# Computing an expert router's gates for three tiles at a time instead of tile by tile

## The chip, the cores and the metric

The kernel runs on one core of a Trainium2 chip. All arithmetic is in float32. The metric is the time of one execution on the device in microseconds (us), the median of several runs. The engines are called as in the profile: PE (TensorE, matrix products), DVE (VectorE), ACT (ScalarE), POOL (GpSimd) and SP (SyncE, which here only issues transfers).

## The reference, cut to what matters

Two layers run on 1024 tokens of 1024 channels each (4 images of 16 by 16). Layer 0 is a convolution-like attention with relative positions. Layer 1 is a causal attention followed by a mixture of eight experts. Only the mixture matters here:

```python
gate_logits = softmax(x @ gate_w + gate_b)            # x: 1024 normalised tokens, 8 experts
selected = gate_logits >= 0.1
weights = gate_logits * selected
weights = weights / where(sum(weights) == 0, 1, sum(weights))
out = sum over e of weights[:, e] * (x @ expert_w[e] + expert_b[e])
```

The kernel does not run every token through every expert. It makes, for each expert, a list of the tokens that chose it, with their weights, gathers those tokens' rows, multiplies them with the expert's matrix and adds the weighted result to the output rows.

## The kernel before, in words

The 1024 tokens are 8 tiles of 128 (`NT = 8`, `P = 128`). The part that matters is the end of the attention and the beginning of the experts, where three things are interleaved on the engines by hand (`tc.manual_schedule()`: each engine executes in the order in which the code issues).

**The output projection as a clock.** `project_out(t, j)` (L894) computes half `j` of tile `t` as 8 products of 128x128 by 128x512 (L898), then DVE adds the result to the residual row `xb` (L900). After each product `one_more()` (L1325) raises the counter `chunks`; I call the products chunks and number them as the code does. Chunk 8 is the last product of tile 3's first half, chunks 9 to 16 are tile 3's second half, 17 to 24 and 25 to 32 tile 4, 33 to 48 tile 5, 49 to 64 tile 6, 65 to 80 tile 7. At a given chunk the table `after` (L1301) starts stages of the gating of earlier tiles:

- stage 0, `normalise` (L1117): layer norm of the tile's rows on DVE and ACT (a square root, L134), and for tiles 0 to 5 a way through memory and back on SP's queue that puts the row into the order that a DVE transpose needs. Tiles 6 and 7 are transposed on PE instead.
- stage 1, `turn_rows` (L1140): the transpose (L179 on DVE, or L1149 on PE with copies L1150 on ACT).
- stage 2, `gate_sums` (L1159): 8 small products into `parts` (L1163), and a DVE copy `sums` (L1165).
- stage 3, `gate` (L1168): one product `pg` (L1171) that adds the four partial sums, then DVE adds the bias and takes the maximum, and ACT makes the exponentials (L1180).
- stage 4, `thresholds` (L1183): ten small DVE instructions, among them the choice `g_keep` (L1188).
- stage 5, `place` (L1197): two products `pp` (L1201, L1202) count, for each token and expert, how many tokens were kept before it (`kept` is the running count over tiles, L1203); DVE turns the count into a list position (L1207 to L1213) and into two 0/1 tables `one` (L1216). Products of one table with token and weight, `entry` (L1224), are made by POOL, for tiles 6 and 7 by DVE.
- stage 6, `enter` (L1233): 8 small products add the tile's entries to `lists` in PSUM (L1235).

**Around tile 7 and the start of the experts.** After chunk 80 the list of expert 0, which doesn't need tile 7, is copied (L1246), spread (L1255) and taken as gather indices (`take_lists`, L1274 to L1277). POOL then issues the gathers of expert 0's rows, four per 128 slots (`fetch`, L1010). Meanwhile `weighted` (L1018) runs tile 7 through expert 0's matrix as it stands: 16 products `dense_pe` (L1025), with tile 7's own stages 2 to 5 at places named in a dictionary (L1528 to L1535). DVE makes the sums that the expert's products need: `T` from the weights (L1384, L1387, L1394), `A`, the transposed gathered rows (L179), and `S` from A (L152 to L155). Each pair of 128 slots is computed with seven half-size products instead of eight (`products`, L1427; L1441). Tile 7's `enter` stands between product 2 and product 3 of expert 0's first pair (L1557), and after product 4 the other seven lists are spread and taken (`last_lists`, L1354).

Tiles in PSUM named by `tr` and `mm` rotate over three banks each, so a product may also wait until the third tile before it has been read.

Of the kernel before, what the change touches and what calls it, by code (L numbers as in the profile page):

```python
# [32 lines left out]
F32 = mybir.dt.float32  # L33
# [6 lines left out]
P = 128  # L40
C = 1024
# [28 lines left out]
def kernel(  # L70
# [57 lines left out]
    def tr(name):  # L128
        return ps.tile([P, HALF], F32, tag="tr", name=name)
# [937 lines left out]
    with ExitStack() as gating:  # L1067
# [38 lines left out]
        nc.vector.memset(ones, 1.0)  # L1106
        kept = l2.tile([P, E], F32, tag="kept", name="kept")
        nc.vector.memset(kept, 0.0)
        kept_short = l2.tile([P, 2], F32, tag="kept_short", name="kept_short")

# [47 lines left out]

        def gate_sums(t, row_T):  # L1159

            parts = tr(f"parts{t}")[:, :P]
            for c in range(NC):
                nc.tensor.matmul(parts[ts(c % Q, 32), :], gw[:, c, :], row_T[:, c, :], start=(c < Q), stop=(c >= Q))  # L1163
            sums = l2w.tile([P, P], F32, tag="parts", name=f"sums{t}", bufs=1)
            nc.vector.tensor_copy(sums, parts)  # L1165
            return sums

        def gate(t, sums):  # L1168

            pg = tr(f"pg{t}")  # L1170
            nc.tensor.matmul(pg[:, :E], sums, quarters, start=True, stop=True)  # L1171
            listed = small.tile([P, E, 2], F32, tag="listed", name=f"listed{t}")
            nc.vector.tensor_copy(listed[:, :, 0], token[:, t : t + 1].to_broadcast([P, E]))
            weight = listed[:, :, 1]
            top = small.tile([P, 1], F32, tag="g_top", name=f"g_top{t}")
            fix = small.tile([P, 1], F32, tag="g_fix", name=f"g_fix{t}")
            keep = small.tile([P, E], F32, tag="g_keep", name=f"g_keep{t}")
            nc.vector.tensor_add(weight, pg[:, :E], gb)
            nc.vector.tensor_reduce(top, weight, AX.X, ALU.max, negate=True)
            nc.scalar.activation(weight, weight, AF.Exp, bias=top)  # L1180
            return listed, top, fix, keep

        def thresholds(listed, top, fix, keep):  # L1183
            weight = listed[:, :, 1]
            nc.vector.tensor_reduce(top, weight, AX.X, ALU.add)
            nc.vector.reciprocal(top, top)
            nc.vector.tensor_scalar(weight, weight, top, None, ALU.mult)
            nc.vector.tensor_scalar(keep, weight, THRESHOLD, None, ALU.is_ge)  # L1188
            nc.vector.tensor_mul(weight, weight, keep)
            nc.vector.tensor_reduce(top, weight, AX.X, ALU.add)  # L1190
            nc.vector.tensor_scalar(fix, top, 0.0, None, ALU.is_equal)
            nc.vector.tensor_add(top, top, fix)
            nc.vector.reciprocal(top, top)
            nc.vector.tensor_scalar(weight, weight, top, None, ALU.mult)
            return listed, keep

        def place(t, listed, keep):  # L1197


            pp = tr(f"pp{t}")  # L1200
            nc.tensor.matmul(pp[:, :E], before, keep, start=True, stop=False)  # L1201
            nc.tensor.matmul(pp[:, :E], ones, kept, start=False, stop=True)  # L1202
            nc.vector.tensor_add(kept, kept, keep)  # L1203
            if t == NT - 2:
                nc.vector.tensor_copy(kept_short, kept[:, :: E - 1])
            slot = small.tile([P, E], F32, tag="place", name=f"place{t}")
            nc.vector.tensor_scalar(slot, keep, -1.0, 1.0, ALU.mult, ALU.add)  # L1207
            nc.vector.tensor_mul(slot, slot, from_end[:, t, :])
            nc.vector.tensor_add(slot, slot, pp[:, :E])
            at = small.tile([P, 3, E], I32, tag="at", name=f"at{t}")  # L1210
            nc.vector.tensor_copy(at[:, 0, :], slot)
            nc.vector.tensor_scalar(at[:, 1, :], at[:, 0, :], 31, None, ALU.bitwise_and)
            nc.vector.tensor_scalar(at[:, 2, :], at[:, 0, :], 5, None, ALU.logical_shift_right)  # L1213
            row, column = (l2w.tile([P, E, 32], F32, tag=f"one{i}", name=f"one{i}_{t}") for i in range(2))
            for i, one in enumerate((row, column)):
                nc.vector.tensor_tensor(  # L1216
                    one,
                    count32.unsqueeze(1).to_broadcast([P, E, 32]),
                    at[:, 1 + i, :].unsqueeze(2).to_broadcast([P, E, 32]),
                    ALU.is_equal,  # L1220
                )
            entry = l2w.tile([P, E, 2, 32], F32, tag="entry", name=f"entry{t}")
            for i in range(2):
                (nc.vector if t >= NT - 2 else nc.gpsimd).tensor_mul(  # L1224
                    entry[:, :, i, :], column, listed[:, :, i].unsqueeze(2).to_broadcast([P, E, 32])
                )
            return row, entry
# [53 lines left out]

        normal, turned_rows, summed, gated, placed = {}, {}, {}, {}, {}

        def stage(n, t):
            if n == 0:
                normal[t] = normalise(t)
            elif n == 1:
                turned_rows[t] = turn_rows(t, normal[t])
            elif n == 2:
                summed[t] = gate_sums(t, turned_rows[t])  # L1290
            elif n == 3:
                gated[t] = gate(t, summed[t])
            elif n == 4:
                gated[t] = thresholds(*gated[t])
            elif n == 5:
                placed[t] = place(t, *gated[t])
            else:
                enter(t, *placed[t])


        after = {  # L1301
            0: (8, 16, 18, 19, 20, 24, 29),
            1: (8, 23, 26, 27, 28, 32, 37),
            2: (19, 30, 33, 34, 35, 39, 44),
            3: (27, 38, 40, 41, 42, 46, 51),
            4: (34, 47, 50, 51, 52, 56, 61),
            5: (50, 61, 63, 64, 66, 69, 74),
            6: (65, 69, 71, 72, 73, 76, 80),
        }
# [15 lines left out]
        def one_more():  # L1325
            nonlocal chunks
            chunks += 1
            for t in after:
                for n, at in enumerate(after[t]):
                    if at == chunks:  # L1330
                        stage(n, t)
            others.get(chunks, lambda: None)()
# [21 lines left out]
        def last_lists(entries):  # L1354
            take_lists(1, E, spread_lists(1, entries))


            pn = tr("pn")
            nc.tensor.matmul(pn[:, :E], ones, kept, start=True, stop=True)
            need = l2.tile([P, E], F32, tag="need", name="need")  # L1360
            nc.vector.tensor_copy(need, pn[:, :E])
            pn0 = tr("pn0")
            nc.tensor.matmul(pn0[:, :2], ones, kept_short, start=True, stop=True)
            nc.vector.tensor_scalar(need[:, :: E - 1], pn0[:, :2], float(LEFT), None, ALU.add)
            most = l2.tile([P, 1], F32, tag="most", name="most")
            nc.vector.tensor_reduce(most, need, AX.X, ALU.max)
            nc.vector.tensor_copy(most_i, most)
# [25 lines left out]
        def fourth_sum(e):  # L1393
            nc.vector.tensor_sub(T[e][2], half(e, 1, 0), T[e][1])  # L1394
# [120 lines left out]
        with tc.manual_schedule():  # L1515
# [3 lines left out]
            for k in range(3):  # L1519
                get(0, k)  # L1520
            y = weighted(
                lambda: gated[NT - 1][0][:, 0, 1:2],
                turned_rows[NT - 1],
# [4 lines left out]
                {  # L1528
                    (0, 3): lambda: stage(2, NT - 1),
                    (0, 4): lambda: (stage(3, NT - 1), first_sum(0)),  # L1530
                    (0, 5): lambda: stage(4, NT - 1),
                    0: lambda: (stage(5, NT - 1), put(0, 0)),
                    (1, 3): lambda: put(0, 1),
# [11 lines left out]
            for e in range(E):  # L1545
# [10 lines left out]
                if e == 0:  # L1556
                    between[2] = lambda: (stage(6, NT - 1), fourth_sum(0), put(0, 2))  # L1557
                    between[3] = lambda: (entries.append(copy_lists(1)), put(0, 3))
# [27 lines left out]
                else:  # L1586
                    between = {
                        1: lambda: nc.sync.dma_start(last_rows[0], out[ts(NT - 1, P), :]),
                        4: lambda: nc.vector.scalar_tensor_tensor(
                            last_rows[0], bias[e], gated[NT - 1][0][:, e, 1:2], last_rows[0], ALU.mult, ALU.add  # L1590
                        ),
# [4 lines left out]
            for j in range(2):  # L1596
# [5 lines left out]
                y = last_rows[0][:, ts(j, HALF)]  # L1602
                nc.vector.scalar_tensor_tensor(y, pe, gated[NT - 1][0][:, E - 1, 1:2], y, ALU.mult, ALU.add)
                nc.sync.dma_start(out[ts(NT - 1, P), ts(j, HALF)], y)
# [69 lines left out]
```

## Time and profile before

| | us |
|---|---|
| median of 3 runs (lowest, highest) | 1237.75 (1236.86, 1240.2) |
| the profiled execution's own time | 1237.34 |
| its span in the profile | 1235.5 |

| stage (us from the span's start) | length | PE busy | DVE busy | ACT busy | POOL busy |
|---|---|---|---|---|---|
| chunks 8 to 80, 661.47 to 742.42 | 80.95 | 78.59 | 57.23 | 28.29 | 9.66 |
| tile 7 and its 16 products, 742.42 to 764.90 | 22.48 | 19.51 | 14.01 | 5.71 | 14.34 |
| expert 0's first five products and the lists, 764.90 to 785.33 | 20.43 | 19.11 | 17.67 | 1.45 | 7.51 |
| the rest, 785.33 to 1235.50 | 450.17 | 444.59 | 255.78 | 57.42 | 204.30 |

The granted PE clock is 1.00 in all four. A row of the timeline gives the start and the length in us, the engine, the source line, the operation, out<-in and the number of merged instructions; in square brackets stands how long the engine was idle before it, and what ended that. A float32 product appears as two records on PE, so "x2" is one product. The end of a product is modelled, and includes a tail that overlaps the next one.

### The profile page before, as it was taken

To read this page: it belongs to the slowest core of one execution; us is meant where nothing else is said; L and a number is where in the kernel's file an instruction comes from. 1 tells how busy PE (TensorE), PEld (TensorE's weight loads), DVE (VectorE), ACT (ScalarE), POOL (GpSimd) and SP (SyncE) were. 2 spreads that over 40 slices of the span, in tenths; PEclk is the share of its full clock that TensorE was granted. 3 is DMA by queue.
4 is the path that set the end of the run, shared out by engine and by line. 5 is a ranking of instruction groups with operands and counts; after the bars stand their busy time and mean duration, and the time that the engine had idled before them with its cause. 6 is when DMAs were issued, how large, how long until landed. Compare 5 with 4: busy or idle time off the path is not lost.

```text
span 1235.5 us, 13332 instructions
## 1 busy us (share of the span) xinstructions
PE 1219.3 (99%) x4796; PEld 631.7 (51%) x4796; DVE 740.5 (60%) x1333; ACT 219.8 (18%) x514; POOL 409.6 (33%) x470
## 2 busy tenths in 40 slices
PE   9999999999999999999999999999999999999998
PEld 5445884788874444444444444444344434434443
DVE  5796636757323666657554867666656556565642
ACT  3310111130001222222222332101201111111110
POOL 0041341354000222223240106436452645363521
PEclk9999999999999999999999999999999999999999
DMA  9002024771220635253483547373855576556442
GB/s 350 23 1 80 7 48 140 254 260 50 68 68 5 180 100 172 91 170 116 134 267 133 205 171 255 89 218 89 239 147 156 111 230 163 152 137 182 100 83 54
DMA packets 94121, 169.77 MB, mean 137 GB/s; under 512 B 11968, under 2 KB 48848, under 8 KB 94048
## 3 DMA queue, kind: packets, MB, share of 16 engines
q1 hardware_dynamic: 75680, 112.68, 28.0%
q0 software_dynamic: 16144, 51.45, 17.4%
q10 hardware_dynamic: 2224, 4.72, 1.1%
q8 instruction: 40, 0.66, 0.2%
q14 instruction: 33, 0.27, 0.1%
HBM read 116.12 MB, written 48.50 MB: 133 GB/s over the span
## 4 chain that ended last, share of the span: by engine, by line
PE 70%; issue 13%; POOL 5%; DMA 4%; DVE 4%; SPq 2%; ACT 1%; POOLq 0%; DVEq 0%; ACTq 0%
PE p L1441 31%; PE pv L657 7%; PE po L898 6%; POOL s_q L855 5%; PE pq_pair L392 4%; PE left L1483 3%; PE pq L311 3%; PE pqk L657 3%; PE pk L423 2%; DMA ln_rows<-ln_rows 2%; PE rest L1497 2%; PE pv L530 2%; PE pT L502 2%; SPq L479 2%; DMA s<-two_T 1%
## 5 line engine op out<-in xcount | busy, mean ns | idle before, releaser
L1010 POOL DMA_INDIRECT w_e_xg<-rows,gather x146 | 156.6, 1073 | 57.3 <-issue 42.0
L1441 PE MATMUL p<-w_e,A 128*128 128x512 f32 x368 | 163.2, 593 | 1.3 <-DVE slot L1276 1.3
L855 POOL TENSOR_TENSOR s_q<-s_q,total 128x128 f32<-128x128 f32 (+1 forms) x128 | 66.0, 546 | 276.8 <-DVE total L852 276.8
L898 PE MATMUL po<-w_p,y_T 128*128 128x512 f32 x256 | 118.5, 605 | 0.0
L1033 POOL DMA_INDIRECT out_dram<-y,add x32 | 57.3, 1792 | 177.6 <-ACT y L1447 113.0
L1441 PEld LDWEIGHTS p<-w_e,A 128*128 128x128 f32 x368 | 69.6, 190 | 89.9 <-issue 89.7
L1441 PE MATMUL p<-T,S 128*128 128x512 f32 x256 | 112.7, 593 | 0.0
L1447 ACT ACTIVATE y<-y,slot 128x512 f32<-128x512 f32 x64 | 46.1, 722 | 330.8 <-DVE y L1455 176.2
L841 ACT ACTIVATE s_q<-s,top 128x256 f32<-128x256 f32 (+1 forms) x128 | 56.6, 443 | 186.3 <-issue 146.9
L657 PE MATMUL pqk<-ln,w_qk 128*128 128x512 f32 x192 | 85.6, 595 | 0.0
L1441 PEld LDWEIGHTS p<-T,S 128*128 128x128 f32 x256 | 48.6, 190 | 60.8 <-issue 60.5
L898 PEld LDWEIGHTS po<-w_p,y_T 128*128 128x128 f32 x256 | 45.9, 190 | 47.9 <-issue 46.9
L179 DVE STREAM_TRANSPOSE A<-w_e_xg 128x1024 f32<-128x1024 f32 x32 | 39.6, 1238 | 48.3 <-DMA w_e_xg<-rows,gather 48.3
L657 PE MATMUL pqk<-T,S_qk 128*128 128x512 f32 x128 | 58.5, 599 | 0.0
L657 PEld LDWEIGHTS pqk<-ln,w_qk 128*128 128x128 f32 x192 | 36.0, 190 | 43.3 <-issue 42.3
L1441 PE MATMUL p<-w_e,S 128*128 128x512 f32 x128 | 57.5, 592 | 0.0
L1441 PE MATMUL p<-T,A 128*128 128x512 f32 x128 | 57.5, 592 | 0.0
L311 PE MATMUL pq<-w_q,xn 128*128 128x512 f32 x96 | 44.5, 599 | 0.3 <-ACT xn L291 0.3
L657 PE MATMUL pv<-w_v,ln 128*128 128x256 f32 x192 | 43.5, 380 | 1.1 <-ACT ln L215 1.1
L1483 PE MATMUL left<-w_e,one 128*32 128x512 f32 x312 | 41.8, 593 | 0.0
L1441 PEld LDWEIGHTS p<-w_e,S 128*128 128x128 f32 x128 | 24.3, 190 | 30.6 <-issue 30.4
L1441 PEld LDWEIGHTS p<-T,A 128*128 128x128 f32 x128 | 24.3, 190 | 30.6 <-issue 30.4
(327 smaller groups left out, 1893.3 us busy)
## 6 DMA issues: line engine op xcount, KB each, us to landing
w_e<-in_expert_w_dram SPq DMA_DIRECT2D x14, 2048.0 KB, 14.6
s_rows<-s_q SPq DMA_DIRECT2D x32, 384.0 KB, 2.4
s_rows<-s_rows SPq DMA_DIRECT2D x128, 96.0 KB, 2.4
w_qk<-in_W_attnT_dram SPq DMA_DIRECT2D x8, 1024.0 KB, 5.8
xn<-in_xT_dram SPq DMA_DIRECT2D x8, 512.0 KB, 5.5
w_q<-in_Wq_dram SPq DMA_DIRECT2D x16, 256.0 KB, 7.6
x_at<-in_x_dram POOLq DMA_DIRECT2D x8, 512.0 KB
w_v<-in_W_attnT_dram SPq DMA_DIRECT2D x2, 2048.0 KB, 11.2
```

The lines of the kernel that those rows point to most:

```text
L179: nc.vector.transpose(row_T[:, :, :slots].rearrange("p c (g j) -> p g c j", j=32), row[:, : slots // 32, :].rearrange("p g (c i) -> p g c ...
L311: nc.tensor.matmul(pq, xn[:, c, ts(t, P)], w_q[kc][:, c, :], start=(c == 0), stop=(c == NC - 1))
L392: nc.tensor.matmul(bank, a[:, c, :], b[:, c, :], start=(c == 0), stop=(c == NC // 2 - 1))
L657: nc.tensor.matmul(bank, stationary(c), moving(c), start=(c == 0), stop=(c == NC // 2 - 1))
L841: nc.scalar.activation(blocks(h, qt), s[:, h, cols].rearrange("p (b f i) -> p b f i", f=Q, i=32), AF.Exp, bias=top[:, qt, h : h + 1], accu ...
L855: nc.gpsimd.tensor_mul(blocks(h, qt), blocks(h, qt), total[:, qt, h : h + 1].unsqueeze(2).unsqueeze(3).to_broadcast([P, 1 + qt, Q, 32]),)
L898: nc.tensor.matmul(po, y_T[:, c, ts(t, P)], w_p[j][:, c, :], start=(c == 0), stop=(c == NC - 1))
L1010: nc.gpsimd.indirect_dma_start(out=row[:, g, :], out_offset=None, in_=table[: (TOK - P) * Q, :] if e in SHORT else table, in_offset=bass.I ...
L1033: nc.gpsimd.indirect_dma_start(out=out[: TOK - P, :] if e in SHORT else out, out_offset=bass.IndirectOffsetOnAxis(ap=add[:slots, e, k : k ...
L1441: nc.tensor.matmul(bank, a[:, c, :], b[:, c, :], start=(c == 0), stop=(c == NC // 2 - 1))
L1447: nc.scalar.mul(y[i][:, ts(j, HALF)], y[i][:, ts(j, HALF)], slot[:, e, 1, 2 * pair + i : 2 * pair + i + 1])
L1483: nc.tensor.matmul(bank[ts(i, 32), :], stationary, w[of][j][:, c, :], start=(c == 0), stop=(c == NC - 1))
```

## The change

Stages 2 to 5 are computed once for the tiles 0 to 2, once for 3 to 5, and for 6 and 7 alone. The partial sums of three tiles lie side by side in one PSUM bank and are copied at once; `pg` still is one product per tile, into one tile; the DVE instructions work on 24 columns instead of 8; the maximum is subtracted by a DVE instruction, and one exponential serves the three tiles. `kept` becomes a table with a row for each tile (each row is the one before it plus that tile's choice), so that one pair of `pp` products serves the group; these additions now stand ahead of the products. The `one` and `entry` tables become a stage of their own, `entries_of` (stage 6), still tile by tile, and `enter` is stage 7. The table of times is written anew, as `at_chunk`: for a chunk, the pairs (stage, tile) that start after it; it is shown with its lines joined.

```diff
-        def gate_sums(t, row_T):
-            parts = tr(f"parts{t}")[:, :P]
-            for c in range(NC):
-                nc.tensor.matmul(parts[ts(c % Q, 32), :], gw[:, c, :], row_T[:, c, :], start=(c < Q), stop=(c >= Q))
-            sums = l2w.tile([P, P], F32, tag="parts", name=f"sums{t}", bufs=1)
+        def gate_sums(tiles):
+            n = len(tiles)
+            parts = tr(f"parts{tiles[0]}")[:, : n * P]
+            for i, t in enumerate(tiles):
+                for c in range(NC):
+                    nc.tensor.matmul(
+                        parts[ts(c % Q, 32), ts(i, P)], gw[:, c, :], turned_rows[t][:, c, :], start=(c < Q), stop=(c >= Q)
+                    )
+            sums = l2w.tile([P, n * P], F32, tag="ye", name=f"sums{tiles[0]}", bufs=3, padded_shape=[P, C])
             nc.vector.tensor_copy(sums, parts)
...
-        def gate(t, sums):
+        def gate(tiles, sums):
...
             nc.vector.tensor_reduce(top, weight, AX.X, ALU.max, negate=True)
-            nc.scalar.activation(weight, weight, AF.Exp, bias=top)
+            if n == 1:
+                nc.scalar.activation(weight, weight, AF.Exp, bias=top)
+            else:
+                nc.vector.tensor_add(weight, weight, top.unsqueeze(2).to_broadcast([P, n, E]))
+                nc.scalar.activation(weight, weight, AF.Exp)
...
-        def place(t, listed, keep):
-            pp = tr(f"pp{t}")
-            nc.tensor.matmul(pp[:, :E], before, keep, start=True, stop=False)
-            nc.tensor.matmul(pp[:, :E], ones, kept, start=False, stop=True)
-            nc.vector.tensor_add(kept, kept, keep)
+        def place(tiles, listed, keep):
+            n, t0 = len(tiles), tiles[0]
+            for i, t in enumerate(tiles):
+                nc.vector.tensor_add(kept[:, t + 1, :], kept[:, t, :], keep[:, i, :])
+            pp = tr(f"pp{t0}")[:, : n * E]
+            nc.tensor.matmul(pp, before, keep.rearrange("p n e -> p (n e)"), start=True, stop=False)
+            nc.tensor.matmul(pp, ones, kept[:, t0 : t0 + n, :].rearrange("p n e -> p (n e)"), start=False, stop=True)
...
-        after = {
-            0: (8, 16, 18, 19, 20, 24, 29),
-            1: (8, 23, 26, 27, 28, 32, 37),
-            2: (19, 30, 33, 34, 35, 39, 44),
-            3: (27, 38, 40, 41, 42, 46, 51),
-            4: (34, 47, 50, 51, 52, 56, 61),
-            5: (50, 61, 63, 64, 66, 69, 74),
-            6: (65, 69, 71, 72, 73, 76, 80),
-        }
+        at_chunk = {
+            8: ((0, 0), (0, 1)), 16: ((1, 0),), 19: ((0, 2),), 23: ((1, 1),), 27: ((0, 3),), 30: ((1, 2),),
+            33: ((2, 0),), 34: ((0, 4),), 36: ((3, 0),), 38: ((1, 3), (4, 0)), 42: ((5, 0), (6, 0)), 44: ((6, 1),),
+            46: ((7, 0), (6, 2)), 47: ((1, 4),), 48: ((7, 1),), 50: ((0, 5),), 52: ((7, 2),), 61: ((1, 5),),
+            63: ((2, 3),), 65: ((0, 6),), 66: ((3, 3),), 68: ((4, 3),), 69: ((1, 6),), 71: ((2, 6), (5, 3), (6, 3)),
+            73: ((3, 6), (6, 4)), 75: ((7, 3), (4, 6), (6, 5)), 76: ((7, 4),), 77: ((5, 6), (6, 6)), 78: ((7, 5),),
+            80: ((7, 6),),
+        }
...
             y = weighted(
...
-                    (0, 3): lambda: stage(2, NT - 1),
+                    (0, 2): lambda: stage(2, NT - 1),
                     (0, 4): lambda: (stage(3, NT - 1), first_sum(0)),
-                    (0, 5): lambda: stage(4, NT - 1),
-                    0: lambda: (stage(5, NT - 1), put(0, 0)),
+                    (0, 6): lambda: stage(4, NT - 1),
+                    0: lambda: put(0, 0),
+                    (1, 2): lambda: stage(5, NT - 1),
                     (1, 3): lambda: put(0, 1),
...
                 if e == 0:
-                    between[2] = lambda: (stage(6, NT - 1), fourth_sum(0), put(0, 2))
+                    between[2] = lambda: (stage(6, NT - 1), stage(7, NT - 1), fourth_sum(0), put(0, 2))
```

In the last dictionaries the key `(j, c)` means after product `c` of half `j` of tile 7's dense product, a lone key after that half, or after that product of expert 0.

## The prediction

> **What bounds the kernel now.** I read the busy times first, then the chain that ended last, then the timelines of PE, DVE and POOL between 661 and 786 us, where all the edits lie.
>
> ```profile
> PE 1219.3 (99%) x4796; PEld 631.7 (51%) x4796; DVE 740.5 (60%) x1333; ACT 219.8 (18%) x514; POOL 409.6 (33%) x470
> ```
> ```profile
> 885.42 96.33 PE p L1441 x224
> ```
>
> PE is never short of work: time can be won only by taking instructions, or idle time, from PE. In the second line, from the chain, 224 records are 112 products of 512 columns in 96.33 us, 0.86 us each: PE's pace undisturbed. From 785.33 us to the end the chain is PE alone, so whatever is won or lost before that moment is carried unchanged to the end. This is PE before it:
>
> ```profile
> 671.63 0.65 PE L1163 MATMUL parts<-row_T,gw 128*32 128x128 f32 x16 [0.46 <-issue]
> 672.21 1.12 PE L898 MATMUL po<-w_p,y_T 128*128 128x512 f32 x2
> 673.17 0.28 PE L1171 MATMUL pg<-quarters,sums 128*128 128x8 f32 x2
> 673.31 4.54 PE L898 MATMUL po<-w_p,y_T 128*128 128x512 f32 x10
> 677.68 0.28 PE L1201 MATMUL pp<-g_keep,before 128*128 128x8 f32 x2
> 677.82 0.37 PE L1202 MATMUL pp<-kept,ones 128*128 128x8 f32 x2
> 678.04 1.96 PE L898 MATMUL po<-w_p,y_T 128*128 128x512 f32 x4
> ...
> 681.94 0.39 PE L1171 MATMUL pg<-quarters,sums 128*128 128x8 f32 x2 [0.30 <-DVE sums L1165]
> ...
> 690.75 0.39 PE L1171 MATMUL pg<-quarters,sums 128*128 128x8 f32 x2 [0.54 <-DVE sums L1165]
> ...
> 715.59 0.39 PE L1201 MATMUL pp<-g_keep,before 128*128 128x8 f32 x2 [0.34 <-DVE g_keep L1188]
> ...
> 729.51 0.39 PE L1201 MATMUL pp<-g_keep,before 128*128 128x8 f32 x2 [0.50 <-DVE g_keep L1188]
> ...
> 752.92 0.39 PE L1171 MATMUL pg<-quarters,sums 128*128 128x8 f32 x2 [0.75 <-issue]
> ...
> 757.51 0.36 PE L1201 MATMUL pp<-g_keep,before 128*128 128x8 f32 x2 [1.52 <-DVE g_keep L1188]
> ...
> 775.29 0.42 PE L1235 MATMUL lists<-entry,one 128*32 128x64 f32 x12
> ```
>
> The brackets hold the waits at the gates: 2.14 us in the projection's chunks (the first five), 2.27 us beside tile 7 (the last two). The last row has none: tile 7's list entries were ready in time. The distance from one start to the next is what a group costs PE: 0.57 us for the eight `parts`, 0.14 for `pg`, 0.36 for a pair of `pp`.
>
> DVE and POOL beside tile 7 and expert 0's first products:
>
> ```profile
> 754.26 2.28 DVE L1384 TENSOR_TENSOR T<-w_e,w_e 128x2048 f32<-128x2048 f32 x1
> ...
> 759.60 0.81 DVE L1216 TENSOR_TENSOR one<-count,at 128x256 f32<-128x256 int32 x2
> 760.44 0.76 DVE L1224 TENSOR_TENSOR entry<-one,listed 128x256 f32<-128x256 f32 x2
> ...
> 763.61 1.25 DVE L179 STREAM_TRANSPOSE A<-w_e_xg 128x1024 f32<-128x1024 f32 x1 [0.69 <-DMA w_e_xg<-rows,gather]
> ...
> 767.56 2.29 DVE L1387 TENSOR_TENSOR T<-w_e,T 128x2048 f32<-128x2048 f32 x1
> ...
> 773.95 0.69 DVE L1450 TENSOR_TENSOR y<-p,U 128x512 f32<-128x512 f32 x1
> ```
> ```profile
> 754.58 2.79 POOL L1010 DMA_INDIRECT w_e_xg<-rows,gather  x1 [0.30 <-issue]
> ```
>
> From 763.61 on DVE works without a break worth naming through S, T, the dense result and p's sums to 774.64; that chain starts when the second gather has landed. One gather issue took 2.79 us, the others about 0.95: it met the 2.28 us sum T.
>
> **Part by part: the projection's chunks.** (1) *Fewer `pp`.* Seven pairs become three: 4 x 0.36 = 1.44 us less. The grouped pairs have 24 columns; 16 more at 0.86/512 us is 0.03 for each of four products, 0.11 back. Sum -1.33. The changed program's order of instructions confirms it: 142 small products of the gates, not 150, with `parts` and `pg` as many as before.
>
> (2) *Fewer interruptions.* A chunk between two small groups takes 0.96 us (672.21 to 673.17), five take 4.37 (673.31 to 677.68): a run costs 0.07 to 0.10 more than its chunks at 0.86. The whole stage says more: 80.95 us, less 2.79 of waits (below), 73 chunks 62.78, parts 4.03, pg 0.98, pp 2.52, six groups of `lists` 2.16 (0.36 each) and the eight transposes of tile 6 0.90, leaves 4.8 for 27 runs, 0.18 each. By the new table there are 16 runs. Eleven fewer at 0.07 are 0.8, at 0.18 2.0; I take 0.15, nearer the stage's figure because it covers all runs: -1.65.
>
> (3) *Waits that go.* Listed are 2.14. Three single chunks before `pg` took, without the listed waits, 1.13, 1.12 and 1.28 where 0.96 is free of waits, so another 0.65 hides there. They should all go: tile 0's transposed row is long ready at chunk 33, and `pg` comes three chunks (2.6 us) after `parts`, not one, while the copy of 384 columns is below 0.7, the price of a 512-column DVE row. Sum -2.8.
>
> (4) *New waits.* `kept` is now added up ahead of its product. At chunk 71 PE has tile 6's `parts`, then the group's `pp`; DVE has the copy of those sums (0.29), then two dependent additions (0.16 each). With 0.05 to 0.08 at the hand-overs and 0.14 for the first `pp` in between, PE waits 0.55. At chunk 42, DVE and ACT need, from `pg` on, about 0.6 for bias, maximum and subtraction, 1.28 for the table, 0.30 for the exponential, 2.1 for `thresholds` (676.02 to 678.09), 0.67 for L900 and 0.36 for two additions, 5.3 in all; PE's six chunks take 5.3. I take 0.2. Sum +0.75. From below this is nothing; from above, DVE has 9.8 us to do between the group's second `pp` and tile 6's `enter` (place 1.3, three `one` pairs 2.3, L900 0.7, tile 6's gate, thresholds and place 4.0, its tables 1.5) and PE 10.0, so that a few delays such as the token copy's beside POOL's `entry` (0.59 us, otherwise 0.16) make 1 to 2 us.
>
> (5) *At nothing:* 79 fewer DVE instructions of mostly 0.16 us and eight fewer ACT table loads of 1.28 us. PE's chunks hide them: DVE is busy 57 of 81 us there, ACT 28. Without the cover they'd be worth some 13 and 10 us. The Trainium skill, "ScalarE: Activation LUTs", section "What ACT_TABLE_LOAD costs", adds a drain of about 1.38 us to each load; that is ACT's time too, and the sum would be the same.
>
> SP's queue keeps its order, and the transfers of stage 0 and the transposes keep their chunks; but the chunks between get cheaper. The nearest case is tile 5: DVE waited 0.88 us for its row (720.01). From chunk 50 its row needs about 12.1 us until it is transposed, and PE asks for it after 13 chunks, one `lists`, and the `parts` of tiles 3 and 4, 13.0 us: hidden, with 0.9 to spare.
>
> Projection: -1.33 - 1.65 - 2.8 + 0.75 = **-5.0**.
>
> **Part by part: tile 7 and expert 0.** I count from the end of chunk 80 (742.42), E. `lists` of expert 0, the indices and POOL's issues follow E as before, so the second gather still lands at E + 21.2. (6) `parts` comes a chunk earlier, `pg` two chunks after it, `pp` six after that: the waits of 0.75 and 1.52 go, and expert 0's first product starts at E + 20.2. (7) Its third needs the second T, which hangs on the gather: done at 769.85, E + 27.4, while PE is there at E + 20.2 + 6.9 = E + 27.1: a wait of 0.35. (8) Tile 7's tables, 1.5 us, stood in DVE's pause before the gather; now they stand behind `y` (ends at 774.64), so they end at E + 33.7. Behind them wait the third T, the second pair's A and the sums that follow; PE wants `lists` after its third product, 3.5 us long, at E + 31.0. It waits 2.75, and `lists` starts at 776.2 in old time instead of 775.29: **+0.9**. The 1.32 us wait before 785.33 follows unchanged.
>
> Of what is moved past other queues: `place` of tile 7 now follows the first A on DVE and so waits for the first gather, but nothing needs it before `y`; POOL has finished its `entry` products before E, so its gather issues are not delayed.
>
> This wait is long. The longest in the gates before, 1.52 us, left the granted clock at 1.00. The Trainium skill, "TensorE: Matmul & The Clock Gate", section "What's actually happening", says that PE's clock halves after an idle window of about 3.4 us; no run here shows that. A window at half clock would add an estimated 1.7 us, and the sum would be 1234.9.
>
> Together -5.0 + 0.9 = -4.1; from the profiled execution's 1237.34, which is 0.41 under the median, **1233.2**.
>
> **The rivals.** *The gather binds less.* If T no longer meets a gather issue, the 1.84 us that the issue was stretched come off E + 21.2, and `lists` with it: 1231.4; if every wait at expert 0 goes, -5.0 - 2.27, 1230.1. For it: T now starts about 1 us earlier after E. Against: issues follow each other every 1.26 us, so T meets another one.
>
> *DVE is short at chunks 71 to 80.* The slack of (4) is used up and 2 us are lost: 1235.2. For it the 9.8 against 10.0; against it, that POOL's 1.20 us `entry` pairs overlap only part of it.
>
> *Slower: more stretched issues.* Place: POOL's first eight gather issues, which set E + 21.2. Each stretched one costs 1.84 and reaches PE undiminished at `lists`; from the third more on (5.5 against 4.1) the change loses. Five more, +9.2, make 1242.4. For it: tile 7's gate is now closer to the issues and the first A follows at once. Against: in the old trace only 2.3 us long DVE instructions did it (issues beside a transpose took 0.95 to 1.04), and only one T lies there.
>
> **How the numbers follow.** A measurement of this kernel can tell about 0.3%, 3.7 us, from no change: below 1234.0 counts as faster. Forecast 0.57 (1231.6 to 1235.0, from the bounds of (2) and (4); 0.45 of it under 1234.0), gather 0.13, DVE short 0.18, stretched issues 0.12. Faster 0.45 + 0.13 = 0.58, same 0.12 + 0.18 = 0.30, slower 0.12. The range reaches from the gather rival, 1230.0, past the DVE rival to 1236.5.
>
> **What would show it.** In the new profile: three `pp` pairs before tile 7; no wait at `pg`; about 0.55 at the second `pp`; none at tile 7's gates; 2 to 3 us at tile 7's `lists`; A from the second gather 21 us after chunk 80. Wrong would be the forecast if chunks 8 to 80 shrink by less than 3 or more than 6.5 us, if the `lists` wait is missing, or if PE waits anywhere after expert 0's first pair.

## The result and the profile after

| | us |
|---|---|
| changed kernel, median of 12 runs (lowest, highest) | 1237.4 (1234.41, 1241.78) |
| kernel before, median of 12 runs on the same chip | 1238.22 (1236.86, 1241.44) |
| ratio, 95% interval | 0.9994 (0.9981 to 1.0006) |
| span of the profiled execution, after (before) | 1235.8 (1235.5) |

No change that can be measured, where 1233.2 was forecast, with 1230.0 to 1236.5 as the range. The two profiled executions, stage by stage:

| | before | after | difference | forecast |
|---|---|---|---|---|
| start of chunk 8 (no edit lies before it) | 661.47 | 664.54 | +3.07 | 0 |
| chunks 8 to 80 | 80.95 | 77.51 | -3.44 | -5.0 |
| end of chunk 80 (E) to expert 0's second pair | 42.91 | 43.46 | +0.55 | +0.9 |
| the rest | 450.17 | 450.29 | +0.12 | 0 |

The busy times of the changed kernel, from its page:

```profile
PE 1216.3 (98%) x4780; PEld 630.9 (51%) x4780; DVE 730.6 (59%) x1254; ACT 208.1 (17%) x502; POOL 410.1 (33%) x470
```

PE is 3.0 us less busy than before, and the span is no shorter: in this pair of profiles what was saved was waited away, 3.07 us of it ahead of chunk 8 (see below) and the rest at new places. PE's timeline after shows these:

```profile
688.75 0.65 PE L1164 MATMUL parts<-row_T,gw 128*32 128x128 f32 x16 [0.61 <-DVE row_T L179]
...
692.00 0.73 PE L1179 MATMUL pg<-quarters,sums 128*128 128x8 f32 x6
...
698.35 0.40 PE L1220 MATMUL pp<-kept,ones 128*128 128x24 f32 x2 [0.23 <-DVE kept L1217]
...
720.70 0.65 PE L1164 MATMUL parts<-row_T,gw 128*32 128x128 f32 x16 [1.14 <-DVE row_T L179]
...
731.22 0.40 PE L1220 MATMUL pp<-kept,ones 128*128 128x24 f32 x2 [0.36 <-DVE kept L1217]
...
739.78 0.43 PE L1256 MATMUL lists<-entry,one 128*32 128x64 f32 x16 [0.28 <-POOL entry L1245]
...
757.01 0.28 PE L1219 MATMUL pp<-g_keep,before 128*128 128x8 f32 x2
...
769.21 3.70 PE L1487 MATMUL p<-T,S 128*128 128x512 f32 x8 [0.44 <-DVE T L1433]
...
775.48 0.42 PE L1256 MATMUL lists<-entry,one 128*32 128x64 f32 x12 [2.56 <-DVE entry L1245]
```

The old waits at `pg` and at `g_keep` are gone, as forecast; so are those at tile 7's gate. The forecast waits are there: 0.23 and 0.36 at the `pp` pairs, 0.44 at the second T, 2.56 at tile 7's lists. Not forecast are the two at `parts`: PE asks for the transposed rows of tiles 2 and 5 before DVE has them. What DVE waited for between 664 and 742 us, first before, then after (us in total, times, longest):

```profile
DVE row_T L179 <- DMA quarters<-rows: 4.4, 2, 3.5
```
```profile
DVE row_T L179 <- DMA quarters<-rows: 19.4, 6, 6.1
```

Two of six transposes waited for their row before; now all six do.

The 3.07 us ahead of chunk 8 are waits of PE far from the change, in layer 0 and at the layer norm behind it. In the profile of before, PE's timeline had none of the first four; the last stood there too, at 1.05. The four, and one more of 0.23 at 621.85, make 2.2 of the 3.07:

```profile
237.85 3.70 PE L444 MATMUL pc<-q,k_q 128*128 128x512 f32 x8 [0.18 <-DVE s L452]
...
263.41 7.17 PE L657 MATMUL pv<-w_v,ln 128*128 128x256 f32 x32 [0.83 <-DMA w_v<-in_W_attnT_dram]
...
271.89 3.69 PE L657 MATMUL pv<-w_v,ln 128*128 128x256 f32 x16 [0.43 <-DVE ln L179]
...
276.11 1.36 PE L211 MATMUL ln_pt<-ident,ln_rows 128*128 128x128 f32 x8 [0.53 <-ACT ln_rows L198]
...
278.53 3.72 PE L657 MATMUL pv<-w_v,ln 128*128 128x256 f32 x16 [1.06 <-ACT ln L215]
```

### The profile page after: what moved, and what is told of

Same layout as the page of the kernel before. It is cut to its first block, busy times and chain, and to the rows that moved or that the text cites. A ratio compares the mean times of both kernels' runs of the same rounds, so it can differ in the third digit from the quotient of the medians.

```text
span 1235.8 us, 13219 instructions
## 1 busy us (share of the span) xinstructions
PE 1216.3 (98%) x4780; PEld 630.9 (51%) x4780; DVE 730.6 (59%) x1254; ACT 208.1 (17%) x502; POOL 410.1 (33%) x470
## 4 chain that ended last, share of the span: by engine, by line
PE 67%; issue 13%; DMA 6%; POOL 6%; DVE 4%; SPq 2%; ACT 1%; DVEq 0%; POOLq 0%; ACTq 0%
PE p L1487 30%; PE pv L657 7%; POOL s_q L855 5%; PE pq_pair L392 4%; PE po L898 3%; PE left L1529 3%; PE pq L311 3%; PE pqk L657 3%; PE pk L423 2%; DMA ln_rows<-ln_rows 2%; PE pv L530 2%; PE rest L1543 2%; PE pT L502 2%; DMA quarters<-rows 1%; SPq L174 1%
## 5 line engine op out<-in xcount | busy, mean ns | idle before, releaser
L898 PE MATMUL po<-w_p,y_T 128*128 128x512 f32 x256 | 115.8, 601 | 0.0
L657 PEld LDWEIGHTS pv<-w_v,ln 128*128 128x128 f32 x192 | 36.2, 190 | 7.9 <-ACT ln L215 1.3
## 6 DMA issues: line engine op xcount, KB each, us to landing
w_e<-in_expert_w_dram SPq DMA_DIRECT2D x14, 2048.0 KB, 12.1
```

What stands on the lines that cost most here:

```text
L657: nc.tensor.matmul(bank, stationary(c), moving(c), start=(c == 0), stop=(c == NC // 2 - 1))
L898: nc.tensor.matmul(po, y_T[:, c, ts(t, P)], w_p[j][:, c, :], start=(c == 0), stop=(c == NC - 1))
```

## The experiments

My theory after the two traces: the gate work saves what was forecast, the rows of tiles 2 and 5 and tile 7's tables take part of it back, and what lies ahead of chunk 8 is scatter between executions. All stages read from the traces (the opening is E to expert 0's second pair):

| run | start of chunk 8 | chunks 8 to 80 | opening |
|---|---|---|---|
| kernel before: first, before_again, before_third | 661.47, 663.41, 663.15 | 80.95, 81.12, 81.02 | 42.91, 41.25, 41.26 |
| changed: first, after_again, after_timed, after_fourth, after_fifth | 664.54, 661.52, 660.55, 661.12, 661.91 | 77.51, 77.03, 77.55, 77.22, 77.00 | 43.46, 43.44, 45.54, 44.92, 45.13 |
| rows_later | 664.02 | 76.07 | 43.59 |
| tables_early | 663.31 | 77.30 | 40.77 |
| both, both_again | 661.40, 662.29 | 76.13, 75.85 | 40.99, 40.54 |
| tile7_alone | 663.28 | 81.08 | 40.77 |
| wait_longer | 662.78 | 77.22 | 47.30 |

### Does the start of chunk 8 follow the kernel? (before_again, after_again)

No edit in either.

> The kernel before, once more, to see what scatters. In the two profiled executions the changed kernel began chunk 8 at 664.54 us and the old one at 661.47, although no edit lies before it; the 3.07 us arose between 232 and 276 us (end of layer 0's value weights and the first layer norm's rows by way of memory). Theory S (scatter of the transfers there): chunk 8 of this run starts anywhere from 661 to 666, not tied to the kernel. Rival P (something in the changed program delays this stage): 661.5 within 0.4 here. Either way chunks 8 to 80 take 80.95 us within 0.3, and from the end of chunk 80 to expert 0's second pair 42.9 within 0.5.

> The changed kernel once more. Theory S: chunk 8 starts anywhere from 661 to 666. Rival P: 664.5 within 0.4 again. Either way chunks 8 to 80 take 77.5 within 0.3 and the stage behind it 43.5 within 0.5.

The start went the other way round: 663.41 for the old kernel, 661.52 for the changed one. Over all 14 executions it lies between 660.55 and 664.54, and the earliest belongs to the changed kernel. The 3.07 us are scatter, and not explained further: the waits at L452, at `w_v` and at the layer norm's rows come and go. after_again's chunks missed their expectation, 77.03 instead of 77.5 within 0.3: its waits at `parts` were 0.46 and 0.92, and the one at the first `pp` pair was missing. The old kernel's opening missed its expectation, 41.25 instead of 42.9; in PE's timeline of before_again

```profile
754.12 0.28 PE L1171 MATMUL pg<-quarters,sums 128*128 128x8 f32 x2
...
757.96 0.36 PE L1201 MATMUL pp<-g_keep,before 128*128 128x8 f32 x2 [0.88 <-DVE g_keep L1188]
```

the wait of 0.75 at tile 7's `pg` is missing and that at `pp` is 0.88, not 1.52. Which of the two is usual was asked once more, with before_third:

> The kernel before a third time, for the two waits at tile 7's gate (pg 0.75, pp 1.52 us in the first profile; none and 0.88 in the second). Theory: the copy of tile 7's sums came 1.4 us late in the first profile by accident; 0 and 0.9 are usual, expert 0's opening takes 41.25 within 0.3, and the sum of the prediction counted 1.4 us too many as won. Rival: 42.9 within 0.3 is usual.

41.26, again no wait at `pg` and 0.88 at `pp`. The profile on which the forecast was made held a delay that two others don't: DVE copied tile 7's `sums` 2.11 us after their `parts` began, in before_again 0.71. What held it stays open.

### Rows asked for later (rows_later)

```diff
-            33: ((2, 0),), 34: ((0, 4),), 36: ((3, 0),), 38: ((1, 3), (4, 0)), 42: ((5, 0), (6, 0)), 44: ((6, 1),),
-            46: ((7, 0), (6, 2)), 47: ((1, 4),), 48: ((7, 1),), 50: ((0, 5),), 52: ((7, 2),),
+            34: ((2, 0), (0, 4)), 37: ((3, 0),), 38: ((1, 3),), 39: ((4, 0),), 43: ((5, 0), (6, 0)), 45: ((6, 1),),
+            47: ((7, 0), (6, 2), (1, 4)), 49: ((7, 1), (0, 5)), 53: ((7, 2),),
...
-            63: ((2, 3),), 66: ((3, 3),), 68: ((4, 3),), 69: ((1, 6),), 71: ((2, 6), (5, 3), (6, 3)),
-            75: ((7, 3), (4, 6), (6, 5)), 76: ((7, 4),), 77: ((5, 6), (6, 6)), 78: ((7, 5),),
+            64: ((2, 3),), 67: ((3, 3),), 69: ((4, 3), (1, 6)), 71: ((2, 6),), 72: ((5, 3), (6, 3)),
+            75: ((4, 6), (6, 5)), 76: ((7, 3),), 77: ((7, 4), (5, 6), (6, 6)), 79: ((7, 5),),
```

The table's lines are joined here.

> The changed kernel, with the group products asked for one chunk later (from 33 to 34 and from 63 to 64, the steps behind them one chunk later too) and tile 5 normalised one chunk sooner (49). Theory: the projection gained 3.4 us and not 5.0 because the rows of tiles 2 and 5, which go to memory and come back, are now asked for before they are there (waits of 0.61 and 1.14 at parts). Then these two waits go, chunks 8 to 80 take 75.7 to 76.3 instead of 77.5, and nothing comes in their place but 0.2 to 0.5 at the pairs of pp. Rival (the transfers merely move with PE, or DVE is short at the end): the waits come back at the second pp, at tile 6's pg or at its lists, and the stage stays at 77.2 to 77.8.

76.07: within the theory's bounds. Tile 2's wait is gone, and all 48 records of `parts` run in one piece; tile 5's shrank from 1.14 to 0.89 only. The timeline of PE:

```profile
687.39 1.52 PE L1164 MATMUL parts<-row_T,gw 128*32 128x128 f32 x48
...
719.86 0.65 PE L1164 MATMUL parts<-row_T,gw 128*32 128x128 f32 x16 [0.89 <-DVE row_T L179]
...
740.09 0.43 PE L1256 MATMUL lists<-entry,one 128*32 128x64 f32 x16 [0.33 <-DVE entry L1245]
```

The rival is there too, but small: 0.33 at tile 6's lists, and 0.35 more than before ahead of the copied list, behind chunk 80 (0.89 for 0.54). So the number was met partly by luck: the two waits at `parts` gave back 0.86 us and not 1.75, and the two at the `pp` pairs (0.23 and 0.36), which were expected to stay, went. That tile 5 was asked for a chunk sooner did nothing, for its statistics still stood on DVE behind tile 4's transpose (DVE's timeline):

```profile
705.66 1.25 DVE L179 STREAM_TRANSPOSE row_T<-quarters 128x1024 f32<-128x1024 f32 x1 [2.52 <-DMA quarters<-rows]
706.83 0.65 DVE L900 TENSOR_TENSOR xb<-xb,po 128x512 f32<-128x512 f32 x1
707.40 0.68 DVE L1114 BATCH_NORM_STATS2 ln_stats<-xb 128x6 f32<-128x512 f32 x1
```

### Tile 7's tables early (tables_early)

```diff
-                    (1, 2): lambda: stage(5, NT - 1),
+                    (1, 2): lambda: (stage(5, NT - 1), stage(6, NT - 1)),
...
-                    between[2] = lambda: (stage(6, NT - 1), stage(7, NT - 1), fourth_sum(0), put(0, 2))
+                    between[2] = lambda: (stage(7, NT - 1), fourth_sum(0), put(0, 2))
```

> The changed kernel, with tile 7's tables (one and entry, 1.5 us of DVE) put back in DVE's pause ahead of the second gather. Theory: the 2.56 us wait at tile 7's lists comes from the tables alone standing behind y; it goes, and from the end of chunk 80 to expert 0's second pair there are 41.0 us (40.6 to 41.3) instead of 43.5. Rival (the gather is the bound, by way of the second A, T and the row sums): the wait moves to the second T or to the second pair's first product, and the stage keeps 42.9 to 43.5; or the tables beside POOL's issues stretch those, and the second gather lands later than 20.9 us after chunk 80.

40.77. The lists follow without a wait, and the second T still waits:

```profile
767.72 3.70 PE L1487 MATMUL p<-T,S 128*128 128x512 f32 x8 [0.39 <-DVE T L1433]
771.35 0.42 PE L1256 MATMUL lists<-entry,one 128*32 128x64 f32 x12
771.70 3.70 PE L1487 MATMUL p<-T,S 128*128 128x512 f32 x8
```

So the place of 1.5 us of DVE work decides over 2.6 us of PE's time.

### Times, the better version, and tile 7 by itself (after_timed, both, tile7_alone)

> The changed kernel, timed in five rounds. Theory: in two profiled executions of each kernel chunks 8 to 80 lost 3.4 to 4.1 us and expert 0's opening gained 0.5 to 2.2, so that about 2.3 us (1.2 to 3.5) are left; the ratio comes out near 0.998 (0.9971 to 0.999). Rival: what scatters ahead of chunk 8 (its start lay between 661.5 and 664.5 us in six executions) goes with the changed program after all; then the ratio is 1.000 again and chunk 8 starts at 664 or later here too.

1235.4 against 1236.35 for the kernel before (12 and 23 runs): 0.9987 (0.9976 to 0.9998), within the expectation, about 1.6 us (0.95 between the medians). The rival is refuted: chunk 8 started at 660.55. But the opening took 45.54, more than in any execution until then; the section on the clock below tells why.

The version with both cures has the edits of rows_later and of tables_early, and

```diff
         others = {
+            42: lambda: first_stats(5),
```

> rows_later and tables_early together, and the first half of tile 5's statistics taken at chunk 42, so that its row leaves 0.6 us sooner. Theory: each mends one of the two places where the change fell short, and they add up: chunks 8 to 80 take 75.3 to 76.1, expert 0's opening 40.6 to 41.3, and the time is 6.0 us (5 to 7) under the kernel before, a ratio of 0.9951 (0.994 to 0.996), 3.7 us under the changed kernel. Rival: DVE is short at the end of the projection, and what parts lose in waits comes back at tile 6's lists and at the copy of the lists (0.33 and 0.35 us more in rows_later); then the chunks take 76.3 or more.

1230.28 against 1236.35, 0.9946 (0.9932 to 0.9961). The opening is 40.99. The chunks take 76.13, a little over the expectation, for a reason of my own making: the statistics placed at chunk 42 (0.69 us) stand on DVE just ahead of the additions to `kept`, and PE waits for these:

```profile
695.87 0.40 PE L1220 MATMUL pp<-kept,ones 128*128 128x24 f32 x2 [0.85 <-DVE kept L1217]
...
717.29 0.64 PE L1164 MATMUL parts<-row_T,gw 128*32 128x128 f32 x16 [0.22 <-DVE row_T L179]
```

For tile 5 they did what they were for: with half of its statistics out of the way of tile 4's transpose, PE's wait for its row is 0.22 instead of 0.89, and in both_again there is none.

Since the six runs lay close together, it was timed again:

> The version with the rows asked for later and the tables early, timed a second time. In its first six runs it lay between 1230.07 and 1230.76 us. Theory: its stages are 76.1 and 41.0, against 81.0 and 41.3 (or 42.9) before, so 5.2 to 6.8 us are won and the ratio is 0.9945 to 0.9958. Rival: the six runs were lucky in what lies ahead of chunk 8 (it started at 661.4, the old kernel's at 661.5 to 663.4), and the ratio comes out at 0.996 or more.

1231.77 against 1237.38, 0.9955 (0.9941 to 0.9969). This version is faster than both kernels, by some 6 us against the one before.

Tile by tile in the projection, with the new placing of tile 7 alone:

```diff
-                    (0, 3): lambda: stage(2, NT - 1),
+                    (0, 2): lambda: stage(2, NT - 1),
                     (0, 4): lambda: (stage(3, NT - 1), first_sum(0)),
-                    (0, 5): lambda: stage(4, NT - 1),
-                    0: lambda: (stage(5, NT - 1), put(0, 0)),
+                    (0, 6): lambda: stage(4, NT - 1),
+                    0: lambda: put(0, 0),
+                    (1, 2): lambda: stage(5, NT - 1),
```

> The kernel before, tile by tile in the projection, with tile 7's steps alone moved: partial sums at (0, 2), thresholds at (0, 6), positions and tables at (1, 2). Theory: this placing with the tables ahead of the gather is worth what tables_early showed, 40.8 us (40.5 to 41.3) for expert 0's opening against 41.25 and 42.91 in two executions of the kernel before, and the chunks keep 81.0 within 0.3: 0.4 to 2.1 us, a ratio of 0.9983 to 0.9997. Rival: the opening hangs on the second gather and not on tile 7's gate, and keeps 41.3 to 42.9.

The opening is 40.77, as expected; against the usual 41.25 that is 0.5 us, which the times do not show: 0.9999 (0.999 to 1.0009), beside the expected 0.9983 to 0.9997.

### The clock behind the wait (wait_longer, after_fourth, after_fifth)

In after_timed PE waited at the lists as before, and then the third product took 5.40 us instead of 3.70:

```profile
771.90 0.42 PE L1256 MATMUL lists<-entry,one 128*32 128x64 f32 x12 [2.56 <-DVE entry L1245]
772.25 5.40 PE L1487 MATMUL p<-T,S 128*128 128x512 f32 x8
```

The table of busy times by stretch of the same execution (from:to and its length, PE, PEld, DVE, ACT and POOL busy, then the granted PE clock, the DMA share and GB/s):

```profile
770.00:772.00 2.00, 0.10 (x7) 0.10 (x10) 1.97 (x6) 0.72 (x1) 0.49 (x1) 1.00 0.67 72
772.00:774.00 2.00, 2.00 (x15) 1.08 (x16) 2.00 (x2) 0.00 (x0) 0.00 (x0) 0.67 0.94 182
774.00:776.00 2.00, 2.00 (x3) 0.73 (x3) 2.00 (x5) 0.00 (x0) 0.00 (x0) 0.50 0.09 21
776.00:778.00 2.00, 2.00 (x6) 0.84 (x5) 1.44 (x2) 0.00 (x0) 0.00 (x0) 0.97 0.00 0
```

The clock was 0.50 from about 772.7 to 776.1, the trace's clock record says for 3.41 us, which costs 1.7. To see whether it belongs to the wait, the wait was made longer:

```diff
-                    between[2] = lambda: (stage(6, NT - 1), stage(7, NT - 1), fourth_sum(0), put(0, 2))
+                    between[2] = lambda: (fourth_sum(0), stage(6, NT - 1), stage(7, NT - 1), put(0, 2))
```

> The changed kernel, with tile 7's tables one DVE instruction further back: behind the third sum T (2.28 us), so that PE's wait at tile 7's lists grows from 2.56 to about 4.8 us. In one of four executions with the 2.56 us wait the granted clock fell to 0.50 for 3.41 us behind it, and the product there took 5.40 us instead of 3.70. Theory: the clock is decided in stretches of 3.41 us whose place against the wait is chance, and falls if PE hardly worked in one of them; a wait of 4.8 us fills one nearly always. Then expert 0's opening takes 43.45 + 2.25 + 1.7 = 47.4 (47.2 to 47.6). Rival: the fall in that execution had another cause; then the clock stays at 1.00 here and the opening takes 45.7 (45.5 to 45.9).

47.30: the theory's number, in one execution. The wait and the slow product behind it, in PE's timeline:

```profile
775.57 0.42 PE L1256 MATMUL lists<-entry,one 128*32 128x64 f32 x12 [4.76 <-DVE entry L1245]
775.92 5.40 PE L1487 MATMUL p<-T,S 128*128 128x512 f32 x8
```

Two further executions of the changed kernel:

> The changed kernel once more, for the spread of its parts. Theory: chunks 8 to 80 take 77.0 to 77.6, expert 0's opening 43.45 or, with the fall of the clock (one time in four to five), 45.2 to 45.6; chunk 8 starts anywhere from 660.5 to 664.6. Rival for the start: 663 or later in most executions of the changed kernel.

> As after_fourth: chunks 77.0 to 77.6, opening 43.45 or 45.2 to 45.6, chunk 8 from 660.5 to 664.6.

Chunks and starts were as expected. The clock fell in both (openings 44.92 and 45.13, slightly under the stated bounds): in three of the changed kernel's five executions, oftener than the one in four or five that was expected. It did not fall in rows_later, which has the same wait, nor in any of the seven executions with the tables early or of the kernel before. So the fall belongs to the wait, by three in six executions with 2.56 us of it, one in one with 4.76 and none in seven with waits of 1.52 at most; wait_longer alone, where chance would have given the same one time in two, shows little. The timed runs agree with the half: of 24 of the changed kernel, twelve have a mean granted clock of 0.997 or 0.998 and took 3.0 and 2.3 us more than the others of their set of twelve; of 34 of the kernel before, two do. The mean is no sharp sign, as after_timed's profiled execution has 0.999.

The fall needs no stretch of 3.41 us without work: a wait of 2.56 cannot fill one. In the 3.41 us ahead of the three falls (after_timed, after_fourth, after_fifth) PE was busy for 0.85, 1.17 and 1.34 us, and in after_fourth the clock fell at 771.45, before the wait had ended. That it goes by a fixed beat the clock record shows: in the four executions with a fall, each fall lasted 3.413 us, and the next change, at the kernel's end, came 457.39 us (once 453.97) after it, 134 (133) times 3.413.

## Why the prediction was wrong, point by point

The means of the table give the account: chunks 81.03 to 77.26, -3.8; opening 41.81 to 44.50, +2.7; together -1.1 us, which agrees with the measured ratios (0.9994 and 0.9987 are 0.7 and 1.6 us) and not with -4.1. Of the 3.0 us between, 1.2 were lost in the chunks (-3.8 for -5.0). In the opening 1.1 are the old kernel's, whose first profile had 42.91 where the mean is 41.81, and 1.05 the fall of the clock (44.50 for 43.45); 0.4 go the other way.

**Right: (1) and (2), fewer products and fewer interruptions, with the 0.65 hidden in (3), in their sum.** Without the listed waits, the first executions' chunks took 80.95 - 2.14 = 78.81 before and 77.51 - 2.62 = 74.89 after: -3.9, where 1.33 + 1.65 + 0.65 = 3.6 was forecast; how the 3.9 divides among them no run shows. The listed 2.14 also went. (4) was sized too high if anything: 0.36 at the second `pp`, nothing at the first in four executions of five. (5) cost nothing, as said. The drain of about 1.38 us that the Trainium skill, "ScalarE: Activation LUTs", section "What ACT_TABLE_LOAD costs", adds to each load shows in no row: in the old profile the load of 1.28 us at 713.07 begins 0.02 us after the ACT instruction before it, and the exponential follows 0.02 us after its end. (7) and (8) came within 0.2 us: 0.44 and 2.56 for 0.35 and 2.75. The second gather's A started at E + 20.9.

**Wrong: "hidden, with 0.9 to spare".** This is the largest miss in the projection: 1.4 to 1.9 us of waits at `parts`, 1.6 on average, against nothing. For tile 5, PE did come 13.0 us after the end of chunk 50 (about 706.6, two chunks of 0.86 after 704.84; `parts` of tiles 3 and 4 ended at 719.56). But the row was there only at 719.40 + 1.25 = 720.65, after 14.1 us and not 12.1. In the timelines of DVE and of SP's queue:

```profile
706.80 1.25 DVE L179 STREAM_TRANSPOSE row_T<-quarters 128x1024 f32<-128x1024 f32 x1 [3.07 <-DMA quarters<-rows]
...
719.40 1.25 DVE L179 STREAM_TRANSPOSE row_T<-quarters 128x1024 f32<-128x1024 f32 x1 [6.13 <-DMA quarters<-rows]
```
```profile
712.22 0.34 SPq L1129 DMA_DIRECT2D rows<-row  x1
714.88 1.74 SPq L174 DMA_DIRECT2D quarters<-rows  x4
```

From SP's issue at 712.22 to the transposed row is 8.4 us, as good as before (8.2). The 2.0 us were lost ahead of it: tile 4's transpose waited 3.07 us for its own row, and tile 5's statistics stood behind it on DVE until 708.54. That this place costs the wait is shown by both and both_again, where half of the statistics came sooner and the wait was 0.22 and none, beside 0.89 in rows_later.

For the delay of tile 4's row, look at ACT; the prediction had looked at SP's queue alone. ACT issues the load of expert 0's first weights, 2 MB (2048 KB): in the old kernel behind tile 3's exponential, 5 us after tile 4's row went out, now 0.28 us before it. The timelines of ACT and SP, first before, then after:

```profile
700.24 0.45 ACTq L121 DMA_DIRECT2D w_e<-in_expert_w_dram  x1
```
```profile
695.23 0.34 SPq L1130 DMA_DIRECT2D rows<-row  x1
698.39 1.74 SPq L174 DMA_DIRECT2D quarters<-rows  x4
```
```profile
693.43 0.42 ACTq L121 DMA_DIRECT2D w_e<-in_expert_w_dram  x1
```
```profile
693.71 0.34 SPq L1129 DMA_DIRECT2D rows<-row  x1
700.13 1.74 SPq L174 DMA_DIRECT2D quarters<-rows  x4
```

From the write to the reads that wait for it there were 3.2 us before and 6.4 after, with the DMA engines 43% and 92% busy meanwhile. It is so in all ten executions with grouped gates (6.3 to 6.8) and in none of the four without (3.1 to 3.2). No run moves the load, so that it is the cause is likely and not shown.

For tile 2 the prediction did not ask. PE came to it 27.05 us after chunk 8's start before (688.52) and 23.6 after, because the gates of tiles 0 and 1 no longer stood in between; its row needed 24.2. Here grouping takes work out of the stretch that covers a trip and puts it behind the request: the saving and the lost cover are the same microseconds. rows_later, with a chunk more of cover, has no wait there; of its 1.2 us in the chunks, 0.7 come from `parts` and 0.4 from the `pp` pairs, against the means of the five executions.

**Wrong: (6), the waits of 0.75 and 1.52 as won.** They did go, but two of three executions of the old kernel have 0.88 in place of 2.27. The sum counted 1.4 us as won that are not usually there to win. One profile had been taken for the rule.

**Wrong in weight: the clock.** The prediction kept the half clock out of its sum, because 1.52 us of waiting had left it at 1.00, and reckoned 1.7 us if it came. It came in three of five executions, at that price: the product behind the wait took 5.40 us for 3.70 twice, and 4.94 where the fall had begun before it. The Trainium skill, "TensorE: Matmul & The Clock Gate", section "What's actually happening", describes a clock that is decided over free-running windows of 3413 ns; the 3.41 us, the whole multiple of it and the chance in it agree. Its condition, an idle window of about 3.4 us, does not: ahead of the three falls PE had worked for 0.85 to 1.34 us of 3.41.

**The rivals.** None was it. One gather issue was stretched, as before (2.44 us), so neither the gather rival nor the slower one came about. DVE was short at chunks 71 to 80 only by the 0.36 at the second `pp`, forecast at 0.55, and by 0.28 at `lists`, where POOL's `entry` had waited for DVE's `one`. The right rival, that PE overtakes the rows' trips through memory, was dismissed in a few lines, and with the trip of one row on the old schedule.

**Ahead of chunk 8** the first comparison of profiles contains +3.07 us that belong to no edit. The prediction had tied its number to one execution; a start that moves by 4 us between executions of one kernel is as large as the whole forecast.

## What to carry to other kernels

When interleaved work is taken out of an engine's stream, list everything that was timed against that stream by counting, and for each transfer compare the new distance in time with the trip as the trace shows it, its queues included: the cover shrinks by what is saved in it. Look also for transfers that another engine now issues sooner, beside the one in question. Keep short work that a later product needs in another engine's pause, not behind its long instructions. And take two or three profiles of the old kernel before a wait in it is counted as a gain.

## What the runs showed of the hardware

The PE clock fell to 0.50 for 3.41 us, in or behind a wait of only 2.56 us, in three of six executions, and behind one of 4.76 us in the one tried; the product that lay wholly in the fall took 1.7 us more. Tile 5's row of 128x1024 float32 took 8.2 to 8.7 us, in all 14 executions, from the issue of its write to its transposed copy by way of memory. Tile 4's, written 0.28 us after the issue of a 2 MB load, took 14.3 us in the changed kernel's first profile (693.71 to 708.05).
